# Two lists of steps per pass for the end of a head pair, in the passes of layer 1 and of layer 0's last block

## The chip, the core and the metric

The kernel runs on one core of a Trainium2 chip. The metric is the device time of one execution in microseconds, the median of several runs. The core has a matrix engine (PE, whose weight loads are shown as PEld), a vector engine (DVE), a scalar engine (ACT), GpSimd (POOL) and a sync engine (SP) that issues DMAs. In this kernel PE, ACT and DVE execute the order that the program writes out by hand, and each executes its own order without skipping.

## The reference

Two graph-attention layers (8 heads of 32 features, 4096 nodes of 256 features, a dense 0/1 adjacency), then one transformer layer whose attention is masked by the same adjacency:

```python
def _gat_layer(x, adj_mat, W, a):
    O = W.shape[-1]
    N = x.shape[0]
    Wh = jnp.einsum('nd,hdo->hno', x, W)
    src = jnp.einsum('hno,ho->hn', Wh, a[:, :O])
    dst = jnp.einsum('hno,ho->hn', Wh, a[:, O:])
    e = jax.nn.leaky_relu(src[:, :, None] + dst[:, None, :], LRELU_SLOPE)
    e = jnp.where(adj_mat[None, :, :] > 0, e, NEG_INF)
    alpha = jax.nn.softmax(e, axis=-1)
    out = jnp.einsum('hnm,hmo->hno', alpha, Wh)
    return jnp.transpose(out, (1, 0, 2)).reshape(N, -1)
h = jax.nn.elu(_gat_layer(x, adj_mat, W1, a1)) + x
out = jax.nn.elu(_gat_layer(h, adj_mat, W2, a2)) + h
...
x = x + out @ w_proj + b_proj          # after masked attention
h2 = layer_norm(x, g2, be2)
ff = jax.nn.gelu(h2 @ w1 + b1) @ w2 + b2
return x + ff
```

## The kernel before

The change lies in the two graph-attention layers (`graph_attention`). The leaky ReLU has two slopes, so the exponential of a score is a product of a factor of the source node and one of the neighbour, with one pair of factors where the sum is positive and another where it is not. A softmax row thus becomes two matrix products: one with the neighbours where a comparison holds, one with those where it doesn't (or with all of them, to subtract from). So a layer needs no exponential per edge, only a matrix of bytes per head that says on which side of the comparison an edge lies, masked by the adjacency.

The work is cut into 256 **passes** `(l, nb, p, g)`: layer `l` (0, 1), block `nb` of 1024 source nodes (4), head **pair** `p` (4), and group `g` of 512 neighbours (8). The eight passes of one `(l, nb, p)` accumulate in six PSUM banks. Below, "pass 7" is the pass with `g = 7`.

- `compare(i)` makes the bytes of pass `i` in a buffer `t8` (`t_p` has three). It has four steps `k` of two instructions of 128x1024, one for each head: ACT (L1122, a sign) for the second head and for a few of the first (the list `more`), DVE (L1124) for the others. A fifth step, `mask`, is one DVE instruction L1137 over all the bytes. `compare(i + 2)` is placed in program position `i`, two passes ahead of its use.
- **Kept-and-false bytes**: in pass 6 of a pair with `apart(i)` true (layer 1 other than its first pair, layer 0's last block other than its last pair, and not in the very last pair), `mask` makes two more tiles (`u8`, shown as `g_adj`, DVE L1132 twice): edges kept by the adjacency for which the comparison is false. Such a pass uses matmuls of 66 columns only and is shorter on PE.
- PE's matmuls of a pass are L1462. While they are written out, a list `side` of other steps is merged in: `beside(steps, since, until)` spreads steps evenly over a share of the pass, and `side` is sorted by these places. This fixes the order of ACT's and DVE's instructions as well as PE's.
- In pass 7, ACT copies the six banks into `ev_broad` (L1472), and `pair_end` appends seven **lists of steps** to `later`:

```python
later.extend([
    [step_load, step_add], [step_scale], [step_subtract], [step_invert, step_divide],
    [step_exp], [step_below, step_above],
    [step_out_and_keep if keeps else step_out],
])
```

These lists turn sums into the layer's output rows. Load is an SP DMA of 256 KB into `e_x` (L743). Add (L1166), scale (L1172), subtract (L1181), invert (L713, L714, L1187), divide (L1191), below (L1200), above (L1204) and out (L1223) run on DVE; exp (L1196) runs on ACT; out also issues a DMA of 256 KB (L1224). The pools of `ev_broad` and `e_x` have one buffer each. In the last pair of layer 0, `step_out_and_keep` (L1210, L1214) takes the place of out and also fills the rows that layer 1's preparation transposes. `take(n)` hands out the next `n` lists, and the loop over passes places them in the part 0.1 to 1.0 of the pass.

- The preparation of layer 1 (features, values, term rows) is spread over passes 2 to 7 of `(0, 3, 3)` and passes 3 and 4 of `(1, 0, 0)`. Beside the last pair, `(1, 3, 3)`, run first steps of the transformer (`handed`, among them norm statistics L1513). SP has no written order outside the beginning: the scheduler orders its DMAs.

Of the kernel before, what the change touches and what calls it, by code (L numbers as in the profile page):

```python
# [723 lines left out]
TILES = ((8, 8, 8, 8), (8, 8, 8, 8))  # L724
# [27 lines left out]
def graph_attention(  # L752
# [111 lines left out]
    def mask_clip(nb, c, i, load=True):  # L864

        v = rows_p.tile([P, G * P, 2], F8, name="adj_8", bufs=5)
        nc.vector.tensor_scalar(
            v.rearrange("p m r -> p r m"),
            loaded.pop((nb, c, i)),
            1.0,  # L870
            -(2.0**-30),
            op0=ALU.min,
            op1=ALU.max,
            saturate=False,
        )
        clipped[nb, c, i] = v.rearrange("p m r -> p (m r)").bitcast(F16)
        if load:
            load_ahead(1)
# [208 lines left out]
    def take(n):  # L1087
        return [step for _ in range(min(n, len(later))) for step in later.pop(0)]
# [268 lines left out]
    for i, (l, nb, p, g) in enumerate(groups):  # L1357
# [7 lines left out]
        def beside(steps, since, until):  # L1365
            for k, step in enumerate(steps):
                side.append((since + (until - since) * (k + 0.5) / len(steps), step))
# [43 lines left out]
        if i == NG - 2:  # L1411
            clips = turns.get(i + 1, []) + clips
        beside([lambda u=u: mask_clip(*u) for u in clips], 0.1, 1.0)
        beside(take(4 if l > 0 and nb == 0 and p == 0 else 1), 0.1, 1.0)
        side.sort(key=lambda step: step[0])
        t8, others = s8.pop(i), u8.pop(i, None)
        tiles = TILES[l][nb]
# [729 lines left out]
def kernel(  # L2147
# [26 lines left out]
    with ExitStack() as scope:  # L2174
        dram = scope.enter_context(tc.tile_pool(name="layers_d", bufs=1, space=DRAM))
        rows = [Rows(nc, [x], [N // P])]
        for l, tiles in enumerate(TILES):
# [18 lines left out]
        ahead = Ahead(nc, norms, rows[2], stage_p, rows_p, w_qkv)  # L2196
        weights = [(gat_w1, gat_a1), (gat_w2, gat_a2)]
        graph_attention(
            tc, adj, rows, mask_d, weights, checks, stage_p, rows_p, ident, ahead.steps()
        )  # L2200
# [53 lines left out]
```

## Time and profile before

| | |
|---|---|
| median of 3 runs | 3152.01 us (3151.06 to 3152.51) |
| the profiled execution | 3150.14 us, span 3148.4 us |
| granted TensorE clock, mean | 0.995 |
| busy: PE, DVE, ACT, POOL | 3081.3, 2784.0, 2690.9, 1195.9 us |
| graph attention | from the start to about 1608 us |
| the eleven pairs from 1071.4 to 1561.4 us | 44.5 us each |

"Busy" is the time in which an engine executes something; overlapping instructions count once. A line of waits reads: engine and line that waited, what ended the wait, microseconds in total, times, longest. A line of the table by stages reads: stretch, its length, then busy time and count of PE, PEld, DVE, ACT and POOL, granted clock, DMA share, GB/s. A line of the timeline reads: start, duration from first to last of merged instructions, engine, line, operation, out<-in, shape, count, and in brackets the idle time before it and what ended that. Instructions of one engine overlap at their ends, so the time from one start to the next is shorter than a duration.

### The profile page before, as it was taken

How to read it: one execution, taken by the hardware profiler on the slowest of the kernel's cores; microseconds unless marked ns; L12 is line 12 of the kernel's file. 1: busy time of each engine (PE TensorE's matmuls, PEld its weight loads, DVE VectorE, ACT ScalarE, POOL GpSimd, SP SyncE). 2: the span in 40 equal slices, each digit the busy share in tenths (PEclk: the TensorE clock that was granted, in tenths of full speed). 3: DMA queues.
4: the chain of work that ended last, by engine and by line, in shares of the span. 5: the costliest groups of instructions: out<-in, count | busy, mean ns of one | idle time of the engine just before them, and what ended most of it. 6: DMA issues, size and time to landing. Idle time of an engine off the chain costs nothing.

```text
span 3148.4 us, 139188 instructions
## 1 busy us (share of the span) xinstructions
PE 3081.3 (98%) x63976; PEld 2708.4 (86%) x63976; DVE 2784.0 (88%) x3140; ACT 2690.9 (85%) x3340; POOL 1195.9 (38%) x538
## 2 busy tenths in 40 slices
PE   6999999999999999999999999999999999999998
PEld 5899999999889999999976888888888888877766
DVE  7999999999989999999986999999999999997220
ACT  6899999999899999999965988898888888886232
POOL 3300000000320000000003988999998899987110
PEclk8999999999999999999999999999999999999999
DMA  8766555430311213111144101011101110013210
GB/s 256 219 198 206 166 185 157 145 90 26 106 50 36 83 56 96 39 59 50 46 125 142 34 21 41 21 34 28 34 21 34 31 28 27 28 39 100 69 34 22
DMA packets 213170, 250.34 MB, mean 80 GB/s; under 512 B 89120, under 2 KB 133664, under 8 KB 212576
## 3 DMA queue, kind: packets, MB, share of 16 engines
q1 hardware_dynamic: 212576, 241.37, 25.6%
q8 instruction: 502, 8.22, 1.1%
q14 instruction: 92, 0.75, 0.1%
HBM read 198.84 MB, written 42.47 MB: 77 GB/s over the span
## 4 chain that ended last, share of the span: by engine, by line
PE 47%; ACT 2%; DVE 2%; POOL 1%; issue 1%; DMA 0%; SPq 0%; DVEq 0%; ACTq 0%; POOLq 0%
PE u_ps L1871 15%; PE u_av L1889 14%; PE u_dn L1889 8%; PE misc L2133 4%; PE misc L2113 3%; ACT t L1122 2%; PE misc L1809 2%; POOL u_both L2025 1%; PE misc L2074 1%; PE misc L1828 1%; DVE t L1124 1%; DVE t L1137 1%; PE misc L1555 0%; DVE u_e L1880 0%; ACT ev_broad L1472 0%
## 5 line engine op out<-in xcount | busy, mean ns | idle before, releaser
L1462 PE MATMUL bank<-vst,t 128*128 128x132 f16 x16384 | 1457.6, 220 | 9.1 <-DVE t L1137 8.8
L2025 POOL TENSOR_TENSOR u_both<-u_e 128x1024 f32<-128x1024 f32 x448 | 1049.5, 2388 | 896.9 <-DMA u_k<-half_d 780.7
L1462 PE MATMUL bank<-vst,mask 128*128 128x132 f16 (+1 forms) x10516 | 1372.6, 206 | 0.0
L1122 ACT ACTIVATE t<-s_b,g_terms 128x1024 int8<-128x1024 f32 x1234 | 1319.2, 1154 | 25.2 <-PE bank L1462 19.5
L1462 PEld LDWEIGHTS <-t 128*128 128x128 fp8e4 x16384 | 1186.6, 96 | 22.4 <-DVE t L1137 12.0
L1880 DVE SCALAR_TENSOR_TENSOR u_e<-u_mask,u_ps 128x1024 f32<-128x1024 uint8 x1024 | 1164.6, 1207 | 13.3 <-ACT u_ps L1878 4.9
L1878 ACT ACTIVATE u_ps<-u_ps 128x1024 f32<-128x1024 f32 x1024 | 1029.8, 1008 | 125.0 <-PE u_ps L1871 36.0
L1462 PEld LDWEIGHTS <-mask 128*128 128x128 fp8e4 x10516 | 920.8, 98 | 0.0
L1137 DVE SCALAR_TENSOR_TENSOR t<-mask,t 128x2048 int32<-128x2048 int32 x256 | 588.2, 2298 | 74.8 <-ACT t L1122 66.3
L1871 PE MATMUL u_ps<-u_q,u_k 128*32 128x512 f16 x8192 | 632.0, 382 | 6.8 <-DVE u_e L1880 4.3
L1889 PE MATMUL u_av<-u_e,u_v 128*32 128x128 f32 x16384 | 597.8, 273 | 0.0
L1889 PEld LDWEIGHTS u_av<-u_e,u_v 128*32 128x32 f32 x16384 | 483.4, 110 | 131.7 <-issue 0.6
L1124 DVE TENSOR_SCALAR t<-s_b,g_terms 128x1024 fp8e4<-128x1024 f32 x814 | 589.6, 756 | 2.7 <-DMA s_b<-s_d 2.7
L1054 POOL TENSOR_TENSOR vst<-g_adj,vst 128x528 f16<-128x528 f32 x16 | 19.8, 1238 | 727.2 <-ACT g_big L1018 682.6
L1889 PE MATMUL u_dn<-u_both,u_ones 128*32 128x128 f32 x7168 | 280.2, 273 | 0.7 <-POOL u_both L2025 0.6
L1871 PEld LDWEIGHTS <-u_k 128*32 128x32 f16 x8192 | 224.5, 95 | 53.2 <-issue 11.5
L1889 PEld LDWEIGHTS u_dn<-u_both,u_ones 128*32 128x32 f32 x7168 | 212.0, 110 | 42.6 <-POOL u_both L2025 1.5
L2120 ACT ACTIVATE u_hid<-misc,n_b 128x512 f32<-128x512 f32 x64 | 43.9, 687 | 140.2 <-PE misc L2113 140.2
L2133 PE MATMUL misc<-u_k,u_hid 128*128 128x256 f32 x512 | 111.8, 379 | 0.0
L2113 PE MATMUL misc<-ln_cols,u_k 128*128 128x512 f32 x256 | 111.3, 592 | 0.5 <-ACT ln_cols L1558 0.5
L2133 PEld LDWEIGHTS misc<-u_k,u_hid 128*128 128x128 f32 x512 | 96.7, 190 | 13.3 <-issue 0.5
L2113 PEld LDWEIGHTS misc<-ln_cols,u_k 128*128 128x128 f32 x256 | 48.6, 190 | 58.5 <-issue 56.7
(176 smaller groups left out, 1822.9 us busy)
## 6 DMA issues: line engine op xcount, KB each, us to landing
g_adj<-in_adj_dram SPq DMA_DIRECT2D x123, 512.0 KB
s_b<-s_d SPq DMA_DIRECT2D x64, 512.0 KB
mask<-mask SPq DMA_DIRECT2D x128, 256.0 KB
u_mask<-mask SPq DMA_DIRECT2D x64, 256.0 KB
mask<-stage SPq DMA_DIRECT2D x48, 256.0 KB
half_d<-u_halves SPq DMA_DIRECT2D x32, 256.0 KB
u_q<-half_d SPq DMA_DIRECT2D x32, 256.0 KB
rows<-e_x SPq DMA_DIRECT2D x31, 256.0 KB
```

The costliest lines, as they stand in the source:

```text
L1122: nc.scalar.activation(to.bitcast(I8), s, AF.Sign, bias=negd, scale=-1.0)
L1124: nc.vector.tensor_scalar(to, s, negd, -1.0, op0=ALU.is_ge, op1=ALU.mult, saturate=False)
L1137: nc.vector.scalar_tensor_tensor(both, m32.unsqueeze(1).to_broadcast(list(both.shape)), SIGNS, both, op0=ALU.bitwise_or, op1=ALU.bitwise_and,)
L1462: nc.tensor.matmul(to, left, right, start=k not in opened, stop=last)
L1809: nc.tensor.matmul(pq, wq_sb[k][:, i * D + c * P : i * D + (c + 1) * P], hn[:, k, :], start=(k == 0), stop=(k == DC - 1),)
L1871: nc.tensor.matmul(ps[r * O : (r + 1) * O, j, :], k_st[c][:, 2 * u + j, at : at + O], q_st[:, h, :], start=True, stop=True,)
L1878: nc.scalar.activation(ps, ps, AF.Exp, scale=SCALE)
L1880: nc.vector.scalar_tensor_tensor(e, mask, 0.0, ps, op0=ALU.not_equal, op1=ALU.mult)
L1889: nc.tensor.matmul(to[j * O : (j + 1) * O, at], lefts[j], es[j // 2][:, j % 2, at], start=first and part == 0, stop=last and part == PARTS ...
L2025: nc.gpsimd.tensor_tensor(both, es_of[i - 1][u], es_of[i][u], op=ALU.add)
L2113: nc.tensor.matmul(ph, w1_sb[:, k, f * P : (f + 1) * P], hn[:, k, :], start=(k == 0), stop=(k == DC - 1),)
L2133: nc.tensor.matmul(po[:, :D], hid[:, f, at : at + P], w2_sb[:, f, :], start=(f == 0), stop=(f == FC - 1),)
```

## The change

Before, a pass takes one list, and the passes of `(1, 0, 0)` take four. Seven lists last for passes 0 to 6 of the next pair, or passes 0 and 1 of `(1, 0, 0)`. After, passes of layer 1 and of the last block of layer 0 take two lists, so that the seven last for passes 0 to 3 (2, 2, 2, 1), and the passes of `(1, 0, 0)` take three (3, 3, 1). The other passes of layer 0 still take one.

```diff
-        beside(take(4 if l > 0 and nb == 0 and p == 0 else 1), 0.1, 1.0)
+        count = 2 if l > 0 or nb + 1 == len(TILES[l]) else 1
+        beside(take(3 if l > 0 and nb == 0 and p == 0 else count), 0.1, 1.0)
```

The condition for `count` is wider than `apart`: it also holds in pair `(0, 3, 3)` and in the last pair.

## The prediction, made before the changed kernel ran

> **What bounds the kernel now.** I read the page's busy shares, then the table by stages, then the waits of the stage that the change touches, then its timeline engine by engine. The page, and the stage from 1071.4 to 1561.4 us (eleven pairs of layer 1):
>
> ```profile
> PE 3081.3 (98%) x63976; PEld 2708.4 (86%) x63976; DVE 2784.0 (88%) x3140; ACT 2690.9 (85%) x3340; POOL 1195.9 (38%) x538
> ...
> 1071.40:1561.40 490.00, 485.50 (x9729) 484.14 (x9727) 463.07 (x496) 477.12 (x507) 0.00 (x0) 1.00 0.19 55
> ```
>
> PE is busy for 485.5 of 490 us: at most 4.5 us lie in PE's idle time here. ACT (477) and DVE (463) are close behind, so moved work has little room. The waits:
>
> ```profile
> DVE t L1137 <- ACT t L1122: 19.4, 44, 0.9
> ACT t L1122 <- PE bank L1462: 11.2, 11, 1.0
> ...
> PE bank L1462 <- DVE t L1137: 4.5, 11, 0.4
> DVE g_adj L1132 <- ACT t L1122: 4.5, 11, 0.4
> ```
>
> Each pair (44.54 us) has one PE stall, on the mask step L1137. PE's timeline shows where: after the last matmul with `g_adj` (kept-and-false bytes), so ahead of pass 7:
>
> ```profile
> 1154.19 0.19 PE L1462 MATMUL bank<-vst,g_adj 128*128 128x66 f16 x1
> 1154.77 0.29 PE L1462 MATMUL bank<-vst,t 128*128 128x132 f16 x2 [0.39 <-DVE t L1137]
> ```
>
> From 1154.19 to 1154.77 where 0.04 is usual: 0.54 us. DVE of the next pair, up to the mask for pass 7, shows the cause:
>
> ```profile
> 1188.59 2.36 DVE L1132 SCALAR_TENSOR_TENSOR g_adj<-t,mask 128x1024 int32<-128x1024 int32 x2 [0.41 <-ACT t L1122]
> 1190.98 2.29 DVE L1137 SCALAR_TENSOR_TENSOR t<-mask,t 128x2048 int32<-128x2048 int32 x1
> 1193.19 0.75 DVE L1124 TENSOR_SCALAR t<-s_b,g_terms 128x1024 fp8e4<-128x1024 f32 x1
> 1193.86 0.42 DVE L1200 TENSOR_SCALAR ev_broad<-ev_broad 128x512 f32<-128x512 f32 x1
> ...
> 1195.52 0.69 DVE L1204 SCALAR_TENSOR_TENSOR ev_broad<-ev_broad 128x512 f32<-128x512 f32 x1
> ...
> 1196.97 2.29 DVE L1137 SCALAR_TENSOR_TENSOR t<-mask,t 128x2048 int32<-128x2048 int32 x1
> ```
>
> The two extra L1132 and then L1200 and L1204 of the pair end all come before the late mask. For passes 2 to 5 the mask ends 1.25, 1.75, 2.25 and 2.75 us before PE starts them (1170.61 to 1186.19, against 1171.86 to 1188.93): early passes have slack, pass 7 none.
>
> [...] here they overlap (L1200 starts at 1193.86, the next L1124 at 1194.19, 0.33 later for a 0.42 instruction), so I price from start to start.
>
> **The change, part by part.** No instruction is added or removed. Start to start, DVE's steps cost: add 1.17 (885.08 to 886.25), scale 0.61, subtract 0.61, invert 0.44, divide 0.63, below 0.33, above 0.60, out 0.60. DVE's pair-end load at the program positions g = 0 to 6 goes from 1.17, 0.61, 0.61, 1.07, 0, 0.93, 0.60 to 1.78, 1.68, 0.93, 0.60, 0, 0, 0. Position g makes the bytes of pass g + 2.
>
> *Early passes, per pair.* In front of L1132 (pass 6), DVE gets 1.78 + 1.68 + 0.93 + 0.60 - (1.17 + 0.61 + 0.61 + 1.07) = 1.53 more. It idles there for ACT by 0.30, 0.29, 0.29, 0.41 = 1.29, which absorbs most. Mask by mask: that for pass 2 comes 0.3 later (0.61 less 0.30) of 1.25 slack; for pass 3, the worst place, 1.1 (0.61 + 1.07 less 0.59 of idle) of 1.75; for pass 4 1.1 of 2.25; for pass 5 0.7, or 1.0 with ACT's delay below, of 2.75. The slack itself shrinks by up to 0.4, since PE loses its stall and ACT doesn't move with it, so pass 3 keeps about 0.3. No stall. L1166 (add) now runs one compare earlier, at about 1166.1, and the last copy of L1472 that it reads ends at 1163.09.
>
> *ACT's exp* (0.54 start to start, also moved) comes after one L1122 of pass 4. It wants to start at 1174.40 in that frame; divide ends just as the mask for pass 3 starts, at about 1174.6, so ACT waits 0.2 to 0.4. ACT's spare is its 1.0 wait on PE, less the 0.44 that a pair shortens by, plus 0.15 of its waits on `e_x` that vanish, as out now runs three passes earlier and the copies L1472 find `ev_broad` free: 0.7, so the wait of exp fits. Behind exp stand the other L1122 of passes 4 to 6; DVE's below waits for exp, but DVE has a mask (2.29) and two L1124 in between.
>
> *Pass 7, per pair.* The distance from mask 6 to mask 7 falls by L1200 and L1204: 5.99 (1190.98 to 1196.97) to 5.06, -0.93. The chain that ends in the stall starts where ACT begins a new round, released by PE's end of pass 5 (the 1.0 wait), and runs through ACT and DVE to the mask for the next pass 7. PE has, from that end to that pass 7, its own work and the stall of the pair before, which lies behind the start. So two successive stalls share what the chain overshoots: 1.08 now, 0.54 each. It becomes 1.08 - 0.93 - 0.15 + 0.2 (1.53 - 1.29 from above) = 0.2, two stalls of 0.1. The gain is 0.44 a pair. Bounds: 0 left (overshoot gone) to 0.25 left (intervals off by 0.3).
>
> *All regular pairs.* Layer 0, block 3: stalls of 0.20, 0.62, 0.56 give 1.2. Layer 1: 0.19, 0.73, 0.55 and eleven of 0.54 give 0.15 + 0.63 + 0.45 + 4.84 = 6.1. Sum **-7.3** (-8.7 to -5.2).
>
> *Seam, (1,0,0), four lists to three.* Stalls of 1.48 (pass 2) and 0.19 (pass 3) now. ACT and DVE there:
>
> ```profile
> 889.48 0.69 DVE L1191 TENSOR_TENSOR ev_broad<-ev_broad,e_inv 128x512 f32<-128x512 f32 x1
> 890.27 0.65 ACT L1196 ACTIVATE ev_broad<-ev_broad 128x512 f32<-128x512 f32 x1 [1.53 <-DVE ev_broad L1191]
> 890.82 8.41 ACT L1122 ACTIVATE t<-s_b,g_terms 128x1024 int8<-128x1024 f32 x8
> ```
>
> Without invert and divide the mask for pass 2 starts at 888.9, not 890.09: -1.2. But then mask (2.21), L1124 (0.66), invert (0.5), L1124 and divide run in the next position, and divide ends at 893.5, not 890.17. ACT, whose exp now stands after two L1122 of pass 3 (889.7), waits 3.9 instead of 1.53; exp (0.55) and three more L1122 (3.1) end at 897.4, the mask for pass 3 (2.29, behind ACT) at 899.74 against 898.30. So pass 2 starts 1.2 earlier, but pass 3 **1.4** later than now. Then ACT's `g_ft` copies at 900.18 come 2.3 later, PE would stall 0.4, and out-and-keep (now about 901 to 901.7) may hold the transposes of pass 3: +0.8. Seam **+2.2** (-0.8 if ACT is not behind, to +3.5).
>
> *(0,3,3)*, where layer 1 is prepared: exp lands between two `g_ft` copies of pass 2 (+0.7); PE stalls of 0.50, 0.67, 0.43 in passes 3 to 5 lose a step in front of them (-1.0): **-0.3** (±0.8).
>
> *(1,3,3)*: DVE has the norm statistics L1513 too (0.67 a pass) and idles only 0.30 ahead of pass 2; the slack of passes 3, 4, 5 is 1.29, 1.33, 1.22. DVE's extra of 0.61 + 1.07 + 0.32 = 2.0 ahead of pass 4, less 0.30 of idle, plus 0.4 of slack lost as above, overruns 1.33 by **+0.8** (0.3 to 1.2).
>
> *DMAs.* Each pair still issues one load and one store of 256 KB, on SP. The store moves three passes earlier; the `e_x` load behind it goes out at 1160.77 and is wanted at about 1184 instead of 1200. `s_b` loads and mask fetches queued behind serve later passes. If the load were late, out alone would wait, with compare steps behind it. Priced at 0; POOL issues none of this.
>
> **Sum**: -7.3 + 2.2 - 0.3 + 0.8 = -4.6. The profiled execution took 3150.14 (span 3148.4), so 3145.5 there; its median of three runs is 3152.01, 1.87 higher: **3147.4**. 0.2% (6.3 us) is about what a measurement of this kernel can tell from no change.
>
> **Rivals.** *All stalls go and the seam costs nothing*: -8.7 - 0.8 - 0.3 + 0.8 = -9, 3143. For it: overshoot of 0.2 is within my error, and L1137's slack elsewhere. Against: ACT's 1.53 wait at the seam, behind a divide that I expect later still.
>
> *ACT becomes the bound (slower)*: exp follows divide within one pass. Each us of that wait adds half a us to each stall. From 1.1 on, nothing is gained in a pair; at 1.6, each of 16 loses 0.25, +4, with seam, preparation and last pair +2.7: +6.7, 3158.7. For it: the 1.53 at the seam. Against: in regular pairs DVE waits for ACT, 44 times, so ACT is not ahead by so much.
>
> *It does not do what it says*: with ACT setting masks 2 to 6, a new stall ahead of pass 3 takes the old one's place: 3152 ± 1.
>
> **How the numbers follow.** Forecast 0.45 (0.37 within 0.2%, 0.08 faster), its own range 3144 to 3152. First rival 0.27, faster. ACT rival 0.20 (0.19 slower). No effect 0.08, same. Faster 0.35, same 0.46, slower 0.19. The range 3143 to 3157 takes in the first rival's centre and the lower part of ACT's.
>
> **What would show it.** Right: PE's waits on L1137 fall from 0.39 to about 0.1 a pair; L1200 stands behind the mask for pass 3; ACT's wait on PE shrinks from 1.0 to about 0.4; the wait of exp on L1191 at the seam grows to about 4. Wrong: a PE stall ahead of pass 3 or 4 in regular pairs, a wait of exp above 1 us in each, or DVE waiting on the load of `e_x`.

## The result, and the profile after

| | before | after |
|---|---|---|
| median, runs beside each other | 3150.97 us (22 runs) | 3146.69 us (22 runs) |
| ratio, 95% interval | | 0.9985 [0.9979, 0.9991] |
| span of the profiled execution | 3148.4 us | 3146.5 us |

The change saves some 4.3 us of the medians. The forecast was 3147.4, and its sum was -4.6. In the traces the graph attention can be compared pass by pass. The table gives the time from PE's first matmul of one pass to that of another:

| from, to | predicted change | before | after | change |
|---|---|---|---|---|
| (0,3,0) to (0,3,3): three pairs | -1.2 | 133.37 | 132.18 | -1.19 |
| (0,3,3) to (1,0,0) | -0.3 | 82.10 | 82.32 | +0.22 |
| (1,0,0) to (1,0,1): seam | +2.2 | 58.38 | 61.38 | +3.00 |
| (1,0,1) to (1,3,3): fourteen pairs | -6.1 | 623.46 | 617.61 | -5.85 |
| (1,3,3), passes 0 to 6 | +0.8 | 39.88 | 39.88 | 0 |
| sum | -4.6 | | | -3.82 |

The two spans differ by only 1.9, because what the change doesn't touch differed too: `(0, 3, 0)` began 1.17 later, and the part from pass 7 of `(1, 3, 3)` on took 0.81 longer.

The busy shares of the page, and the stage of the eleven pairs (same columns as before), now 485.30 us long:

```profile
PE 3081.9 (98%) x63976; PEld 2709.4 (86%) x63976; DVE 2781.7 (88%) x3140; ACT 2691.3 (86%) x3340; POOL 1195.8 (38%) x538
```

```profile
1073.40:1558.70 485.30, 484.60 (x9728) 483.86 (x9725) 460.46 (x496) 477.25 (x508) 0.00 (x0) 1.00 0.20 57
```

The same work (ACT still 477) fits into a shorter stage: 4.5 us of PE's idle time have become 0.7. The waits of this stage (engine and line that waited, what ended it, total, times, longest; L1462 of before is L1463 now):

```profile
DVE t L1137 <- ACT t L1122: 20.7, 22, 1.9
ACT t L1122 <- PE bank L1463: 8.1, 11, 0.9
PEld L1463 <- DVE t L1137: 1.4, 6, 0.3
```

PE's line of 4.5 us is gone; its weight load waits 0.3 at most, six times. ACT's wait on PE has gone from 1.0 to 0.74 on average. DVE no longer waits ahead of the kept-and-false bytes (L1132). What is left stands ahead of pass 7 in every second pair. PE's timeline there, from the last matmul of pass 6 to the first of pass 7:

```profile
1199.81 0.19 PE L1463 MATMUL bank<-vst,g_adj 128*128 128x66 f16 x1
1200.13 0.29 PE L1463 MATMUL bank<-vst,t 128*128 128x132 f16 x2
```

0.32 us from start to start where about 0.04 is usual. A stall is counted here from start to start, less what is usual; the idle time that a line gives in brackets is some 0.15 shorter. The stalls that are left are 0.23 to 0.32 long, and the pairs between have none. DVE ahead of it:

```profile
1190.34 2.36 DVE L1132 SCALAR_TENSOR_TENSOR g_adj<-t,mask 128x1024 int32<-128x1024 int32 x2
1192.74 2.29 DVE L1137 SCALAR_TENSOR_TENSOR t<-mask,t 128x2048 int32<-128x2048 int32 x1
1194.95 2.73 DVE L1124 TENSOR_SCALAR t<-s_b,g_terms 128x1024 fp8e4<-128x1024 f32 x4
1197.79 2.29 DVE L1137 SCALAR_TENSOR_TENSOR t<-mask,t 128x2048 int32<-128x2048 int32 x1
```

Between the masks for passes 6 and 7 only the four comparisons remain: 5.05 us instead of 5.99.

At the seam, ACT's and DVE's timelines show exp waiting for divide with six comparisons behind it, and the mask for pass 3 waiting for the first three of those:

```profile
893.79 0.65 ACT L1196 ACTIVATE ev_broad<-ev_broad 128x512 f32<-128x512 f32 x1 [3.82 <-DVE ev_broad L1191]
894.34 6.33 ACT L1122 ACTIVATE t<-s_b,g_terms 128x1024 int8<-128x1024 f32 x6
```

```profile
893.01 0.69 DVE L1191 TENSOR_TENSOR ev_broad<-ev_broad,e_inv 128x512 f32<-128x512 f32 x1
...
897.59 2.29 DVE L1137 SCALAR_TENSOR_TENSOR t<-mask,t 128x2048 int32<-128x2048 int32 x1 [1.96 <-ACT t L1122]
```

PE idles for 2.60 us, and then something comes that the prediction doesn't have. The two groups of transposes in the timeline of PE start 2.02 apart, where they start 1.15 apart in before:

```profile
899.94 0.29 PE L1463 MATMUL bank<-vst,t 128*128 128x132 f16 x2 [2.60 <-DVE t L1137]
...
900.48 0.88 PE L991 MATMUL turn<-ident,g_rows 128*128 128x128 f32 x4
...
902.50 1.10 PE L991 MATMUL turn<-ident,g_rows 128*128 128x128 f32 x4
```

The table by stages of this stretch says why (the number after POOL's busy time is PE's granted clock):

```profile
898.00:900.40 2.40, 0.46 (x8) 0.47 (x9) 2.40 (x2) 2.40 (x3) 0.00 (x0) 1.00 0.00 0
900.40:901.50 1.10, 1.10 (x13) 1.03 (x10) 1.10 (x4) 1.10 (x2) 0.00 (x0) 0.62 0.00 0
901.50:902.50 1.00, 1.00 (x14) 1.00 (x13) 1.00 (x3) 1.00 (x2) 0.00 (x0) 0.50 0.01 1
902.50:903.60 1.10, 1.10 (x9) 1.04 (x8) 0.85 (x2) 0.72 (x2) 0.00 (x0) 0.50 0.99 203
903.60:904.20 0.60, 0.60 (x11) 0.60 (x9) 0.60 (x1) 0.56 (x2) 0.00 (x0) 0.61 0.59 132
904.20:906.00 1.80, 1.80 (x22) 1.55 (x20) 1.54 (x2) 1.48 (x7) 0.00 (x0) 1.00 0.54 123
```

From 0.7 us after the end of the stall, PE ran at half clock for 3.4 us (900.66 to 904.07). Pass 3 of `(1, 0, 0)` took 12.74 us instead of 11.12.

### The profile page after: what moved, and what is told of

It reads as the page before. It is cut to its first block, busy times and chain, and to the rows that moved or that the text cites. A ratio compares the mean times of both kernels' runs of the same rounds, so it can differ in the third digit from the quotient of the medians.

```text
span 3146.5 us, 139193 instructions
## 1 busy us (share of the span) xinstructions
PE 3081.9 (98%) x63976; PEld 2709.4 (86%) x63976; DVE 2781.7 (88%) x3140; ACT 2691.3 (86%) x3340; POOL 1195.8 (38%) x538
## 4 chain that ended last, share of the span: by engine, by line
PE 50%; ACT 1%; POOL 1%; DVE 1%; issue 0%; DMA 0%; SPq 0%; DVEq 0%; POOLq 0%; ACTq 0%
PE u_ps L1872 15%; PE u_av L1890 14%; PE u_dn L1890 8%; PE misc L2134 4%; PE misc L2114 4%; PE bank L1463 3%; PE misc L1810 2%; POOL u_both L2026 1%; PE misc L2075 1%; PE misc L1829 1%; ACT t L1122 1%; PE misc L1556 0%; DVE u_e L1881 0%; DVE t L1137 0%; DVE t L1124 0%
## 5 line engine op out<-in xcount | busy, mean ns | idle before, releaser
L1463 PE MATMUL bank<-vst,t 128*128 128x132 f16 x16384 | 1457.2, 220 | 4.9 <-DVE t L1137 4.1
L1463 PE MATMUL bank<-vst,mask 128*128 128x132 f16 (+1 forms) x10516 | 1373.2, 206 | 0.0
L1463 PEld LDWEIGHTS <-t 128*128 128x128 fp8e4 x16384 | 1187.1, 96 | 17.2 <-DVE t L1137 6.7
L1463 PEld LDWEIGHTS <-mask 128*128 128x128 fp8e4 x10516 | 921.3, 98 | 0.0
```

What stands on the lines that cost most here:

```text
L1463: nc.tensor.matmul(to, left, right, start=k not in opened, stop=last)
```

## The experiments

The theory after the result: in regular pairs the gain comes from shortening DVE's queue between masks 6 and 7; three lists at the seam cost more than four, because exp then stands in the same position as the divide it needs. Open were the cause of the 0.3 us that are left, and whether the drop of the clock belongs to the stall. The rivals are stated with each run. All ratios are to the kernel before, run beside them. Times of runs vary by 3 to 6 us from one to the next; so for small effects I use the ways in the trace, one profiled execution for each kernel. They repeat well: the kernels that leave the seam as it was have 58.38 or 58.39 there.

| kernel | ratio [95%] | (0,3,3) to (1,0,0) | seam | fourteen pairs |
|---|---|---|---|---|
| before | | 82.10 | 58.38 | 623.46 |
| after | 0.9985 [0.9979, 0.9991] | 82.32 | 61.38 | 617.61 |
| four at the seam | 0.9973 [0.9963, 0.9984] | 82.34 | 58.39 | 617.66 |
| three at the seam alone | 1.0011 [1.0004, 1.0017] | 82.12 | 60.29 | 623.91 |
| three lists per pass | 1.0194 [1.0180, 1.0208] | 84.47 | 58.38 | 669.34 |
| out in position 6 | 0.9975 [0.9966, 0.9985] | 81.99 | 58.38 | 617.60 |
| shift by one | 1.0013 [1.0007, 1.0020] | 81.77 | 58.39 | 627.70 |
| exp late at the seam | 0.9976 [0.9967, 0.9985] | 82.35 | 57.86 | 617.70 |
| less ACT, pass 2 | 0.9997 [0.9989, 1.0005] | 82.32 | 58.38 | 622.29 |
| both of these | 0.9992 [0.9984, 1.0001] | 82.33 | 57.84 | 622.32 |
| less ACT, pass 1 | 0.9971 [0.9961, 0.9982] | 82.35 | 58.38 | 615.48 |
| exp late and less ACT, pass 1 | 0.9966 [0.9954, 0.9978] | 82.32 | 57.85 | 615.54 |

**Two lists, but four at the seam.** Only one half of the change is kept:

```diff
-        beside(take(3 if l > 0 and nb == 0 and p == 0 else count), 0.1, 1.0)
+        beside(take(4 if l > 0 and nb == 0 and p == 0 else count), 0.1, 1.0)
```

> Two lists per pass as in the changed kernel, but four (not three) in the passes of (1,0,0). Theory (the seam loses because exp waits on ACT for divide and holds the bytes of pass 3): ACT's wait at exp goes back from 3.8 to about 1.5 us, the PE stall ahead of pass 3 from 2.7 to 0.2, that ahead of pass 2 from 0.3 back to 1.5, and PE keeps its full clock in pass 3. From the start of pass 0 of (1,0,0) to that of (1,0,1) 58.4 us as before, not 61.4. About 3.0 us faster than the changed kernel, 7 faster than the kernel before. Rival (the 3.0 us come from two lists per pass in the pairs around the seam, not from the three at it): the stretch stays at about 61 us.

Median 3142.23 us against 3150.74. The seam has before's 58.39 and its stalls of 1.47 and 0.20 again, and the regular pairs keep their gain. So the seam's three lists are a plain loss, of 3.0 us in the profiled execution of after, and the two-list passes a gain by themselves.

**Three at the seam alone.** The other half, against the kernel before:

```diff
-        beside(take(4 if l > 0 and nb == 0 and p == 0 else 1), 0.1, 1.0)
+        beside(take(3 if l > 0 and nb == 0 and p == 0 else 1), 0.1, 1.0)
```

> Only the seam is changed: three lists in the passes of (1,0,0), one everywhere else. Theory: 3.0 us slower than the kernel before, all of it between the start of (1,0,0) and (1,0,1), with ACT's wait at exp near 3.8 us, a stall of about 2.7 us ahead of pass 3 and half the TensorE clock for some 3.5 us after it; all other pairs as before, 0.54 us of stall each. Rival (the seam is slow only because DVE and ACT arrive at it in another state in the changed kernel): less than 1 us slower.

Median 3153.94 us, 3.2 more than before. The regular stalls of 0.54 are all there (the last of them is 0.94). At the seam exp waits 3.80 and pass 3 has its stall of 2.74, as in after, but this time the clock stayed full (table by stages behind that stall):

```profile
900.00:901.40 1.40, 1.40 (x27) 1.39 (x25) 1.32 (x3) 1.40 (x2) 0.00 (x0) 1.00 0.07 16
```

Pass 3 took 11.66 us, 0.54 more than before, most of it 0.30 of wait for a late `g_ft` copy (L1000). The way is 1.91 longer than before, not 3.00. So a stall of 2.74 cost about 1.1 more at the seam of after, where a clock of 0.50 followed it, than here, where the clock stayed at 1.00. That the drop belongs to the stall is shown only in part here; the next run takes it up.

**Three lists per pass.** One number is changed, with four at the seam:

```diff
-        count = 2 if l > 0 or nb + 1 == len(TILES[l]) else 1
+        count = 3 if l > 0 or nb + 1 == len(TILES[l]) else 1
```

> Three lists per pass in all passes that have two in the changed kernel, four at the seam. This puts divide, exp and below into one pass in 17 pairs. Theory (exp must not follow divide within a pass, since ACT then waits for DVE): ACT waits about 3.4 us at exp in every pair. Its own work of 43.4 us in a pair leaves 0.7 to spare, so a pair becomes some 46.7 us long instead of 44.1, with a PE stall of about 2 us, most likely ahead of pass 3: 30 to 45 us slower than the kernel before. Rival (only the number of steps behind the kept-and-false bytes matters, so the earlier the better): no stall is left, about 8 us faster than before.

Median 3212.36 us, 61.6 more than before. Each regular pair now has what the seam has in after; the waits from 1069 to 1589 us, with eleven waits of exp, show the whole chain, and the table by stages what followed two of its stalls, one ahead of 1160.4 and one ahead of 1257.1:

```profile
DVE t L1137 <- ACT t L1122: 53.4, 44, 2.4
ACT ev_broad L1196 <- DVE ev_broad L1191: 39.7, 11, 3.6
...
PE bank L1463 <- DVE t L1137: 27.2, 16, 2.6
```

```profile
1161.50:1164.00 2.50, 2.50 (x30) 2.50 (x28) 2.18 (x4) 2.50 (x3) 0.00 (x0) 0.50 0.31 69
```

```profile
1258.00:1260.50 2.50, 2.50 (x53) 2.50 (x51) 2.19 (x4) 2.50 (x3) 0.00 (x0) 1.00 0.25 57
```

Exp waits 3.6 a pair, the mask waits for ACT, PE for the mask: the mechanism of the seam, repeated. Of its 18 stalls of 2.17 to 2.75 us ahead of pass 3, ten were followed by a pass of 7.08 to 7.30 us, and eight by one of the usual 5.70. Both lengths of stall are on both sides. The first table has a clock of 0.50 behind the stall ahead of 1160.4, the second 1.00 behind the one ahead of 1257.1, the longer of the two. What sets them apart was not shown. Ten times 1.5 us is 15 us, about what 61.6 is above the upper end of the expectation.

**Out behind the mask for pass 7.** This asks whether the rest of 0.3 us is set by DVE's sum of work ahead of mask 7: the output step, 0.60, is put behind it (four at the seam).

```diff
-        count = 2 if l > 0 or nb + 1 == len(TILES[l]) else 1
+        count = 1
+        if l > 0 or nb + 1 == len(TILES[l]):
+            count = (2, 2, 2, 0, 0, 0, 1, 0)[g]
```

> As the kernel with four lists at the seam, but the seventh list (out) runs in pass 6 as in the kernel before; two lists in passes 0, 1 and 2. Theory (what is left of the stall, 0.27 us in every second pair, is the sum of DVE's steps ahead of the kept-and-false bytes less its idle time): 0.60 us fewer stand in front of them, the copies of the banks wait 0.15 us again for out, so no stall ahead of pass 7 is left. 1.5 to 2.5 us faster than the kernel with four at the seam, about 9 us faster than the kernel before. Rival (ACT's chain with its exp sets the rest): 0.27 us stay in every second pair, and the time is that of the kernel with four at the seam.

Nothing came of it: the stalls stay at 0.23 to 0.31 in every second pair, the fourteen pairs at 617.60 against 617.66. DVE's timeline says where the 0.60 went, at the mask for pass 5, first after, then this kernel:

```profile
1185.96 2.29 DVE L1137 SCALAR_TENSOR_TENSOR t<-mask,t 128x2048 int32<-128x2048 int32 x1 [0.21 <-ACT t L1122]
```

```profile
1181.42 2.29 DVE L1137 SCALAR_TENSOR_TENSOR t<-mask,t 128x2048 int32<-128x2048 int32 x1 [0.82 <-ACT t L1122]
```

DVE got there 0.60 earlier and waited 0.61 longer for ACT's bytes. Up to this mask it is ACT that sets the time.

**One more list in position 0 only.** This asks whether it matters what is moved past the kept-and-false steps, or only how much stands behind them:

```diff
-        count = 2 if l > 0 or nb + 1 == len(TILES[l]) else 1
+        count = 1
+        if l > 0 or nb + 1 == len(TILES[l]):
+            count = 2 if g == 0 else 1
```

> Two lists in position 0 of a pair only, then one per position (seam as before): below and above move from position 5 to 4, so ahead of the kept-and-false steps, out from 6 to 5, exp from 4 to 3. Theory (a step that moves ahead of the kept-and-false steps pays only where DVE or ACT idles there, and positions 3 and 4 have only 0.41 us of idle): the distance from mask 6 to mask 7 shrinks by just 0.33, while exp and below and above come earlier in the chain by up to 1.4; overshoot about 1.6 in two pairs, stall about 0.8 a pair instead of 0.54, 3 to 4 us slower than before. Rival (only the number of DVE steps between the kept-and-false steps and mask 7 counts, 0.93 to 0.60): 0.17 to 0.33 saved in each of 16 pairs, 3 to 5.6 us faster than before.

Median 3155.27 us against 3150.77. The stalls ahead of pass 7 are 0.82 to 0.87 in every pair, as the theory had it; PE's timeline:

```profile
1200.40 0.29 PE L1465 MATMUL bank<-vst,t 128*128 128x132 f16 x2 [0.73 <-DVE t L1137]
```

The edit moves steps the same way as the change, but less far, and loses time. Behind the kept-and-false steps 0.33 is saved, while below and above (0.93) come in front of them, behind a mask that waits 1.45 for ACT. So it isn't enough to move steps away from mask 7; what they are moved in front of decides.

**Exp late at the seam.** In `(1, 0, 0)`, three lists in position 0; then invert and divide in the first 0.9 of position 1 and exp alone at its end; the rest in the first 0.6 of position 2:

```diff
-        beside(take(4 if l > 0 and nb == 0 and p == 0 else count), 0.1, 1.0)
+        if l > 0 and nb == 0 and p == 0:
+            if g == 1:
+                beside(take(1), 0.1, 0.9)
+                beside(take(1), 0.94, 0.96)
+            else:
+                beside(take(3), 0.1, 0.6 if g == 2 else 1.0)
+        else:
+            beside(take(count), 0.1, 1.0)
```

> Two lists in regular pairs; in (1, 0, 0) three lists in position 0, then invert and divide in the first 0.9 of position 1 and exp alone at its end, below, above and out-and-keep in the first 0.6 of position 2. Theory (what the three lists cost at the seam is ACT's wait for divide in front of exp, with the comparisons queued behind it): exp waits about 0, no stall of 2.7 ahead of pass 3, the granted clock stays at 1.00; stalls of about 0.3 and 0.2 against 1.47 and 0.20 with four lists: the way from (1, 0, 0) to (1, 0, 1) is 57.2 us against 58.39 with four and 61.38 with three, 1.2 us faster than four lists at the seam. Rival (late out-and-keep holds the transposes of pass 3): these wait 1 to 2 us, the way is 58.4 us or more, no gain against four lists.

The stall ahead of pass 3 is gone, the one ahead of pass 2 is 0.32, the clock stays at 1.00. Exp still waits 1.37 for divide, against the expectation, but no comparison of pass 3 is behind it any more, so PE doesn't wait for it. The rival was right in part; PE's timeline shows the transposes held by out-and-keep:

```profile
897.40 0.66 PE L991 MATMUL turn<-ident,g_rows 128*128 128x128 f32 x4 [0.32 <-DVE g_rows L1210]
```

With that and a `g_ft` wait, pass 3 takes 11.98 us, 0.86 more than with four lists. Stalls of 1.35 saved, 0.86 given back: the seam takes 57.86, 0.53 less, not 1.2. The cost of three lists lay in where exp stood, as the theory says. The held transposes and the `g_ft` wait together come to about what the prediction's term for them was, 0.8, but here and not in after.

**One comparison of pass 2 from ACT to DVE.** If ACT's queue sets the rest, less work on ACT should remove it (two lists, four at the seam; `more` lists the first head's comparisons that ACT does):

```diff
             more = (3, 7, 11, 15, 19, 23, 27)
+            if (l, nb, p) not in ((1, 0, 0), (1, 3, 3)):
+                more = (3, 7, 15, 19, 23, 27)
```

> Two lists, four at the seam, and in every pair with kept-and-false bytes one comparison of pass 2 (the first head's in the fourth step) runs on DVE instead of ACT. Theory (the 0.23 to 0.31 us that are left ahead of pass 7 in every second pair are set by ACT's queue: its copies of six banks, then comparisons without a pause up to the bytes of pass 5): ACT's bytes for pass 2 are ready 1.04 us earlier, DVE has idled 1.5 to 1.8 us there and takes 0.66 of work into that; the stalls, 2.2 us in all, go: 2 us faster than four lists at the seam alone. Rival (the sum of DVE's work ahead of mask 7 sets them): 0.66 more per pair, 0.3 more stall a pair, 4 to 5 us slower than four lists at the seam alone.

The opposite: in layer 1 the stalls are now 0.24 to 0.27 in one pair and 0.61 to 0.70 in the next, the fourteen pairs take 622.29, so 4.6 longer. I had misread a line: the wait of 1.5 to 1.8 on ACT belongs to the mask for pass 1, not pass 2. Behind that mask DVE has no idle time until the divide, so divide came 0.66 later, and ACT, 1.04 ahead, only waited for it in front of exp (ACT's timeline):

```profile
1172.72 0.65 ACT L1198 ACTIVATE ev_broad<-ev_broad 128x512 f32<-128x512 f32 x1 [1.69 <-DVE ev_broad L1193]
```

From exp on, ACT's queue is then later than without the edit. The sum of stalls in two pairs grew from 0.27 to about 0.9, one comparison of DVE (0.66). Thus the chain runs through both queues: DVE from the mask for pass 1 to divide, then ACT from exp to the bytes of pass 5, then DVE to mask 7. With both edits (exp late as well), the seam takes 57.84 and the pairs 622.32, so the two effects add up:

> The late exp at the seam together with the comparison of pass 2 moved to DVE. If both theories hold, the two gains lie in different pairs and add: 1.2 + 2.2 = 3.4 us faster than four lists at the seam, about 3138.8 beside 3151 before. If either rival holds, its loss shows alone in its own pairs.

Median 3148.21 us, 2.6 below before and not the expected 3138.8: the gain at the seam shows, and so does the loss in the pairs.

**One comparison of pass 1 from ACT to DVE.** The same edit, one pass earlier, ahead of the mask at which this chain starts:

```diff
-                more = (3, 7, 15, 19, 23, 27)
+                more = (3, 11, 15, 19, 23, 27)
```

> As the kernel with two lists and four at the seam, but in every pair with kept-and-false bytes one comparison of pass 1 (made in position 7 of the pair before, where ACT also copies the banks) runs on DVE instead of ACT. With the comparison of pass 2 moved, exp came to wait 1.69 for divide: DVE between the mask for pass 1 and divide has no idle time. Theory (both queues are tied, and both start a pair from ACT's last byte of pass 1, for which DVE idles 1.5 to 1.8 us): DVE takes the 0.66 into that idle time, the mask for pass 1 starts about 1.0 earlier, everything behind it on both engines too, the stalls of 0.23 to 0.31 ahead of pass 7 go: about 2.2 us faster than without the move, way from (1, 0, 1) to (1, 3, 3) 615.7 against 617.66. Rival (DVE's sum alone, as with the comparison of pass 2): about 0.6 more in two pairs, way about 622, 5 us slower.

The stalls ahead of pass 7 are gone, all of them. The stage of eleven pairs and the waits of the pairs from 1069 to 1553 us:

```profile
1073.40:1558.70 485.30, 485.30 (x9761) 485.30 (x9758) 467.95 (x507) 468.53 (x497) 0.00 (x0) 1.00 0.19 56
```

```profile
ACT t L1124 <- PE bank L1465: 15.7, 11, 1.4
DVE t L1139 <- ACT t L1124: 12.7, 33, 0.8
```

PE is busy for 485.30 of 485.30 us, and no wait of PE is in the list. The mask for pass 1, which waited 1.80 or 1.53 for ACT in after, waits 0.75:

```profile
1156.50 2.29 DVE L1139 SCALAR_TENSOR_TENSOR t<-mask,t 128x2048 int32<-128x2048 int32 x1 [0.75 <-ACT t L1124]
```

So DVE takes the 0.66 into that wait, and both queues start the chain earlier. That ACT simply has less to do doesn't explain it: the comparison of pass 2 took as much work off ACT, and time was lost. The fourteen pairs take 615.48 (expected 615.7). In exchange the last pair, `(1, 3, 3)`, has stalls of 0.07 to 0.08 ahead of its passes 3 and 4, and takes 40.05 instead of 39.88.

**Both together**, the late exp and this comparison:

> The late exp at the seam together with the comparison of pass 1 moved to DVE. The late exp took the way from (1, 0, 0) to (1, 0, 1) from 58.39 to 57.86: the same again, so 0.5 us faster than the kernel beside it on this chip, whichever theory holds for the regular pairs; if the stalls ahead of pass 7 go too, the last pair starts at about 1552 less whatever the start differs, and the time is some 11 us below before.

Median 3140.20 us against 3151.31 of before, the fastest of all: seam 57.85, pairs 615.54. In the traces the way from `(0, 3, 0)` to `(1, 3, 3)` is 887.59 us, against 893.49 in after and 897.31 in before.

## Why the prediction was right, and where not

- **Regular pairs, -7.3: right, measured -7.0.** Stalls that share what the chain overshoots, 0.2 in two pairs, is what happens: 0.27 in one, none in the next. The distance from mask 6 to mask 7 fell by 0.94 (-0.93 predicted), L1200 stands behind the mask for pass 3, and no new stall came ahead of passes 3 to 5.
- **What sets the rest: half named.** The prediction had the chain start at ACT's round and run through ACT and DVE, but only its DVE part was used for the size. DVE's lead up to the mask for pass 5 is worth nothing (out in position 6), DVE's work ahead of divide counts in full (pass 2), and work taken off ACT pays where the chain starts (pass 1).
- **Exp waits 0.2 to 0.4 a pair: wrong, 0.** Divide (0.68 us from 1175.14) ends 0.1 us before exp starts at 1175.92, right behind a comparison: a near tie. So ACT's wait on PE fell to 0.74, not to 0.4. The rival in which ACT becomes the bound turns on this wait; it comes about with three lists per pass, where exp and divide share a position. (That rival reckons with 16 regular pairs; there are 17, three in layer 0 and fourteen in layer 1.)
- **Seam, +2.2: right in sign and mechanism, 0.8 too small in the profiled execution.** The term of 1.4 for the later start of pass 3 is confirmed: 20.20 us from the start of `(1, 0, 0)` against 18.81, +1.39. Exp's wait of 3.82 is the predicted 3.9. The term of 0.8 for what follows failed as it was put: the first transposes started at 900.48, before out-and-keep had run (901.12), and weren't held. In its place stood half clock (0.50 for 3.41 us), which the prediction doesn't have, and pass 3 grew by 1.62. With three at the seam alone and full clock it grew by 0.54, of which 0.30 is the `g_ft` wait that the term has at 0.4. So the term is too large without the drop of the clock and too small with it, and the 2.2 lies between the two outcomes, 1.91 and 3.00.
- **(0,3,3), -0.3: measured +0.22**, inside its ±0.8. Stalls of before shrank from 0.67 to 0.32 and from 0.43 to nothing, but out now falls among the preparation steps, where it takes 1.63 us instead of 0.69, and a stall of 0.53 on L1036 came ahead of 831.2.
- **(1,3,3), +0.8: wrong, 0.** The slack of passes 3, 4 and 5 shrank to 0.28, 0.19 and 0.24, but not below nothing. The step that failed is the overrun of 1.33 by 2.0 less 0.30 plus 0.4: too long by 1.0. The 0.4 of lost slack wasn't there: the mask for pass 1 starts 2.11 us after PE begins the pair, against 2.10 before. And from that mask to the one for pass 4, DVE takes 18.20 us instead of 17.06, so 1.14 more and not 1.7. In before, the mask right behind the comparison of 1574.05 starts 0.84 after it (1574.89); in after, with a step of the pair end between the comparison of 1565.55 and its mask, it is 0.66 and then 0.62, so the step adds 0.44 here and not its 0.61. Where the pair just before has no stall either (comparison of pass 1 moved; exp late), stalls of 0.05 to 0.08 do appear here.
- **DMAs, priced at 0: right.** Out starts at 1184.40 right behind a comparison, without a wait for the load of `e_x`.
- The terms' errors of +0.3, +0.5, +0.8 and -0.8 leave +0.8 in the sum, no more than what one of the untouched parts of the two profiled executions differs by. That the median came within 0.7 us of the forecast is partly luck: two of the errors cancel, the seam's depends on whether the clock drops, and the median of before came out 1.04 below the 3152.01 that the forecast started from.

## What to carry to other kernels

When two engines hand bytes to a third in written order, find the chain through both queues before moving work: a step moved into the front engine's idle time cost nothing here, and the same step one pass later cost 0.66 us in two pairs. Don't place a step of one engine in the same slot as the step of another that it needs, if others' work is queued behind it; here the place of an exp of 0.65 us made a stall of 2.7 us. Don't price a stall of PE by its length alone: behind the one of 2.74 us at the seam of after PE ran at half clock for 3.41 us, and pass 3 took 1.08 us more than in three at the seam alone, where the stall was as long and the clock stayed at 1.00.

## What the runs showed of the hardware

Idle gaps of PE of 2.03 us (ahead of 1160.39, three lists per pass) and 2.60 us (ahead of 899.94, after) were followed by half clock, a granted clock of 0.50; in after it lasted from 900.66 to 904.07, 3.41 us. Behind two other gaps of 2.60 us (ahead of 1257.09, three lists per pass; ahead of 898.72, three at the seam alone) the clock was 1.00, and so it was behind the one of 1.34 us at the seam of before (the stall of 1.48, ahead of 892.43). So the length of the gap doesn't settle it in these runs: the clock fell behind one of 2.03 and stayed full behind two of 2.60. What does settle it was not shown; there is one profiled execution of each kernel.

At the seam, pass 3 took 12.74 us with half clock (after) and 11.66 us without it (three at the seam alone), 1.08 us more on top of a stall of the same length. With three lists per pass, ten of the passes behind such a stall took 1.4 to 1.6 us more than the usual 5.70.
